# A four-layer graph network on one core: the second layer's input transposed by VectorE and through DRAM, the attention sources in another node order, the third layer's sum on GpSimd, and a new plan

## The chip, the cores and the metric

The kernel runs on one core of a Trainium2 chip. The core has five engines that run side by side and meet through semaphores: PE (TensorE, matrix products and their weight loads), DVE (VectorE), ACT (ScalarE), POOL (GpSimd) and SP (SyncE, which here only issues DMAs). The metric is the device time of one launch in microseconds, the median over the runs shown. One launch works through all 32 graphs.

## The reference, cut to what matters

Each of the 32 batch elements is a graph of 512 nodes with 128 features. All share one 0/1 adjacency `adj` (512x512, symmetric, with self loops). Four layers follow each other, each with a residual and a LayerNorm:

```python
x = _layernorm(x + _L0_gnn_ref(x, adj, ...))   # attention: softmax(leaky(s_i + d_j) + mask) @ (x W), leaky 0.3
x = _layernorm(x + _L1_gnn_ref(x, adj, ...))   # attention, then elu
x = _layernorm(x + _L2_gnn_ref(x, adj, ...))   # diag(A) x W[0] + offdiag(A) x W[1] + bias, A = rows of adj, softmaxed
x = _layernorm(x + _L3_gnn_ref(x, adj, ...))   # y = ((adj + I) x) W + bias; y / max(|y|, 1e-12)
```

The LayerNorm is `(x - mean) / sqrt(var + 1e-5)` over the 128 features. So each layer ends in 512 inverse square roots for each graph, and layer 3 in 512 more for its norm.

## The kernel before, in words

Names carry the layer as a digit (`pt1`, `nrm2`) and the graph as `@b`; lines are those of the profile.

**Tiling.** A graph's x is a tile of 128 partitions by 512: four chunks of 128 nodes side by side. Nearly all of the work is cut into *units*: small functions, each of which issues a few instructions on one engine. A table `PLAN` gives each unit and graph a place in one long order, `STARTS` does so for the work done once. The order is written out by the program as it stands, and each engine takes its own instructions in that order; semaphores hold an instruction back until its operands are there. The numbers in `PLAN` are places, not times (2648 of them before, 2980 after). Each tile is taken from a stock of its kind (`sq`: 30 tiles, `ps`: 6 banks of PSUM, and so on) when the first unit of that graph names it, and goes back after the last.

**Layers 0 and 1 (attention).** x has to be transposed first, so that features lie on the partitions. For layer 0, graphs 1 to 31 come in from DRAM by `lb` (four DMAs of short runs, L156), and DVE finishes the transposition in 32x32 blocks (`tr0`, L160). Graph 0, and layer 1 of every graph, is transposed by PE (`pt`, L167, four products with the identity) and copied out of PSUM by ACT (`xt`, L171). `ph` (PE, L179) gives xW with the source and target scores, `ex` (ACT, L183) their exponentials, and `h` (ACT, L189) the scaled rows. The score of the source has to lie along the free axis of every partition: for 27 of the 32 graphs DVE turns it (`rt`, L214), four small DMAs write it to DRAM (`rw`, L220), and one DMA reads it back to all partitions (`rb`, L224); for the other five PE does it (`pr`, L209). `al` (DVE, L236, four instructions of 128x512) forms the masked weights, `po` (PE, L196, 32 products for each layer) applies them. `rs`, `v0`, `lr`, `elu` (DVE) and `v1`, `exp` (ACT) finish the layer; `add` (POOL, L267) adds the residual.

**Layers 2 and 3 (aggregation).** `xh` (ACT, L273) and `xl` (POOL, L277) split x in a rounded part and the rest, `py` (PE, L284) multiplies both with the adjacency, `y` (ACT, L288) copies out, `po2` or `po3` (PE, L298, L299, L311) multiply with the weights. In layer 2 `v2` (DVE, L305) scales by 1/degree and adds `xb`, which is x plus the bias (POOL, L292). In layer 3 `v3` adds the bias (DVE, L315), `sq` squares and sums (ACT, L321), `ssp` takes the inverse root (POOL, L325 and L326), and `rr0` to `rr3` scale and add the residual (DVE, L333).

**The end of every layer.** `bn` (DVE, L340 and L342) gives mean and variance, `ms` (ACT, L346) turns the sign of the mean, `pw` (POOL, L350 and L351) raises the variance to the power -1/2 and multiplies, and `nrm` (ACT, L356) scales and shifts in four instructions. For example:

```python
nc.gpsimd.tensor_tensor(rn[:, 0], mv[:, :, 1], mhalf, op=ALU.pow)
nc.gpsimd.tensor_mul(rn[:, 1], mv[:, :, 0], rn[:, 0])
```

**Beginning and checks.** `e`, `am`, `m`, `mp` make the mask `em` and its transposes `mt` (float) and `mp` (bf16, in PSUM); `cva` copies `mt` to the two matrices of layers 2 and 3, and `cvd` corrects their diagonals. `de`, `dv` and `lp` test the assumptions under which this fast path holds, and `out_d` to `out_c` read out a flag at the end.

Of the kernel before, what the change touches and what calls it, by code (L numbers as in the profile page):

```python
# [18 lines left out]
P = 128  # L19
# [7 lines left out]
def kernel(  # L27
# [49 lines left out]
    an, em, mt = square("an"), square("em"), square("mt")  # L77
    eh = square("eh", BF16)
# [47 lines left out]
    kind("sq", 30, "x1 x2 x3 x4 o0 o1 o2 o3 t t3 xb y2 y3 xt0 xt1 xt2 tr0 tr1 tr2", plain([P, N]))  # L126
# [8 lines left out]
    kind("ss", 6, "ss", plain([P, NCH]))  # L135
    kind("rb", 4, "rb0 rb1", plain([P, N]))
# [21 lines left out]
    @unit("tr0", "sw0", "xt0")  # L158
    def _(b, sw, xt):
        nc.vector.transpose(xt, sw)  # L160

    for k in range(3):

        @unit(f"pt{k}", f"x{k}", f"pt{k}")
        def _(b, xk, p):
            for c in range(NCH):
                nc.tensor.transpose(p[:, c * P : (c + 1) * P], xk[:, c * P : (c + 1) * P], ident)  # L167

        @unit(f"xt{k}", f"pt{k}", f"xt{k}")
        def _(b, p, xt):  # L170
            nc.scalar.copy(xt, p)  # L171

    for k in range(2):
# [33 lines left out]
        def _(b, p, k=k):  # L207
            for c in range(NCH):
                nc.tensor.transpose(p[:, c * P : (c + 1) * P], exps[:, 2 * b + k, 0, c : c + 1].to_broadcast([P, P]), ident)  # L209
# [91 lines left out]
    @unit("v2", "po2", "xb", "o2")  # L301
    def _(b, p, xb, o):
        for c in range(NCH):
            cols = slice(c * P, (c + 1) * P)
            nc.vector.scalar_tensor_tensor(o[:, cols], p[:, cols], rdeg[:, c : c + 1], xb[:, cols], op0=ALU.mult, op1=ALU.add)  # L305

# [28 lines left out]
    for k in range(4):  # L335
# [8 lines left out]
        @unit(f"ms{k}", f"mv{k}")  # L344
        def _(b, mv):
            nc.scalar.mul(mv[:, :, 0], mv[:, :, 0], -1.0)  # L346

        @unit(f"pw{k}", f"mv{k}", f"rn{k}")
        def _(b, mv, rn):
            nc.gpsimd.tensor_tensor(rn[:, 0], mv[:, :, 1], mhalf, op=ALU.pow)  # L350
            nc.gpsimd.tensor_mul(rn[:, 1], mv[:, :, 0], rn[:, 0])  # L351
# [6 lines left out]

    @unit("st", "x4")
# [683 lines left out]
```

## Time and profile before

| | us |
|---|---|
| three runs | 580.44, 582.84, 582.96 (median 582.84) |
| the profiled execution | 582.73 |
| its span, first to last instruction | 581.0 |
| what lies around the span | 1.7 |
| busy: PE / DVE / ACT / POOL | 547.7 / 526.0 / 503.6 / 427.0 |

Busy times are the time in which at least one instruction of the engine was under way. Neighbours overlap in their pipelines, so the mean duration of a short instruction is longer than what it adds: four `nrm` instructions of 492 ns each take 1.55 us together. Group rows give `busy, mean ns of one`, and after the bar the idle time of the engine just before them, with what ended it.

### The profile page before, as it was taken

Reading aid. Unit: us, or ns where it says so; the run is one execution under the profiler, and the core shown is the slowest. Engines: PE = TensorE matmul, PEld = TensorE weight load, DVE = VectorE, ACT = ScalarE, POOL = GpSimd, SP = SyncE. Lnnn points to the kernel's source line nnn. Section 1 sums busy time; section 2 is a strip of 40 time slices with the busy share of each in tenths; the row PEclk is TensorE's granted clock in tenths of the full one; section 3 lists DMA queues with packets and bytes.
Section 4 is the critical chain, followed back from the end, with each engine's and each line's share of the span. In section 5 each row is a group of like instructions: output and inputs, shape, how many; then the busy total and the mean of one; then the engine's idle time right before and its main releaser. Section 6 shows DMA issues by size and latency. Waiting matters only on the chain.

```text
span 581.0 us, 13866 instructions
## 1 busy us (share of the span) xinstructions
PE 547.7 (94%) x4200; PEld 516.1 (89%) x4200; DVE 526.0 (91%) x2005; ACT 503.6 (87%) x1653; POOL 427.0 (73%) x578
## 2 busy tenths in 40 slices
PE   7799999899999999999999999999999999999980
PEld 6689999899999999999999989898998999998860
DVE  2688979899999999999998999999999999779674
ACT  4555598798989899999999889899988999998996
POOL 3151685787868787777878579776887779789985
PEclk9788999999999999999999999999999999999995
DMA  6616022323434334352432343332201111000013
GB/s 188 130 38 128 19 60 70 92 65 83 99 77 101 77 70 110 92 117 55 104 78 76 83 97 74 66 101 73 75 20 38 55 38 38 20 2 20 1 37 113
DMA packets 111296, 41.84 MB, mean 72 GB/s; under 512 B 69872, under 2 KB 103792, under 8 KB 111216
## 3 DMA queue, kind: packets, MB, share of 16 engines
q1 hardware_dynamic: 110640, 40.57, 29.2%
q8 instruction: 35, 0.57, 0.4%
q14 instruction: 45, 0.37, 0.2%
q10 hardware_dynamic: 576, 0.33, 0.2%
HBM read 32.38 MB, written 8.50 MB: 70 GB/s over the span
## 4 chain that ended last, share of the span: by engine, by line
DVE 35%; PE 33%; ACT 16%; POOL 5%; SPq 4%; issue 3%; DMA 2%; ACTq 0%; DVEq 0%; POOLq 0%
PE ps L196 16%; DVE al L236 12%; ACT sq L356 8%; PE ps L284 7%; DVE st L340 6%; PE ps L179 4%; DVE sq L333 3%; DVE sq L305 2%; SPq L156 2%; DVE mv L342 2%; DVE sq L243 2%; ACT hp L189 2%; PE ps L167 2%; PE ps L311 2%; DVE sq L253 2%
## 5 line engine op out<-in xcount | busy, mean ns | idle before, releaser
L196 PE MATMUL ps<-hp,al 128*128 128x129 f32 x2048 | 251.2, 279 | 6.4 <-DVE al L236 4.4
L196 PEld LDWEIGHTS ps<-hp,al 128*128 128x128 f32 x2048 | 243.1, 195 | 10.0 <-issue 3.1
L356 ACT ACTIVATE sq<-sq,rn 128x128 f32<-128x128 f32 x512 | 209.5, 492 | 12.8 <-POOL rn L351 12.6
L350 POOL TENSOR_TENSOR rn<-mv,mhalf 128x4 f32<-128x4 f32 x128 | 134.7, 1053 | 22.1 <-DVE mv L342 15.4
L236 DVE SCALAR_TENSOR_TENSOR al<-rb,exps,mp 128x512 f32<-128x512 f32 x216 | 145.5, 734 | 1.6 <-DMA rb<-rd 1.5
L340 DVE BATCH_NORM_STATS2 st<-sq 128x6 f32<-128x128 f32 x512 | 109.0, 273 | 4.2 <-POOL sq L267 4.1
L277 POOL TENSOR_TENSOR xr<-sq,xr 128x512 fp32r<-128x512 f32 x64 | 83.1, 1302 | 15.1 <-ACT xr L273 13.5
L189 ACT ACTIVATE hp<-ps,exps 128x128 f32<-128x128 f32 x256 | 87.8, 421 | 0.2
L179 PE MATMUL ps<-we,sq 128*128 128x131 f32 x512 | 73.5, 277 | 3.1 <-ACT sq L171 2.0
L179 PEld LDWEIGHTS ps<-we,sq 128*128 128x128 f32 x512 | 66.0, 190 | 5.9 <-ACT sq L171 2.6
L284 PE MATMUL ps<-off,xr 128*128 128x512 f32 x256 | 67.3, 405 | 1.8 <-ACT hp L189 1.5
L284 PE MATMUL ps<-a3t,xr 128*128 128x512 f32 x256 | 67.2, 405 | 0.7 <-ACT sq L249 0.7
L284 PEld LDWEIGHTS ps<-off,xr 128*128 128x128 f32 x256 | 45.7, 188 | 11.4 <-ACT hp L189 1.9
L284 PEld LDWEIGHTS ps<-a3t,xr 128*128 128x128 f32 x256 | 45.9, 188 | 10.2 <-ACT sq L249 1.0
L267 POOL TENSOR_TENSOR sq<-sq,x 128x512 f32<-128x512 f32 x32 | 42.3, 1323 | 15.6 <-DVE sq L253 10.4
L292 POOL TENSOR_TENSOR sq<-sq,bias_b 128x512 f32<-128x512 f32 x32 | 41.6, 1300 | 14.3 <-ACT sq L356 11.6
L333 DVE SCALAR_TENSOR_TENSOR sq<-sq,ss,sq 128x128 f32<-128x128 f32 x128 | 47.6, 413 | 3.7 <-POOL ss L326 3.6
L267 POOL TENSOR_TENSOR sq<-sq,sq 128x512 f32<-128x512 f32 x32 | 41.7, 1306 | 11.3 <-DVE sq L261 10.6
L298 PE MATMUL ps<-w,sq 128*128 128x128 f32 x256 | 49.5, 275 | 0.0
L299 PE MATMUL ps<-w,sq 128*128 128x128 f32 x256 | 49.5, 275 | 0.0
L342 DVE BATCH_NORM_AGGREGATE mv<-st 128x2 f32<-128x9 f32 x512 | 48.9, 155 | 0.0
L171 ACT COPY sq<-ps 128x512 f32<-128x512 f32 x65 | 37.8, 584 | 11.2 <-PE ps L167 10.9
(91 smaller groups left out, 832.9 us busy)
## 6 DMA issues: line engine op xcount, KB each, us to landing
rb<-rd SPq DMA_DIRECT2D x54, 256.0 KB
x<-in_x_dram SPq DMA_DIRECT2D x32, 256.0 KB
out_dram<-sq SPq DMA_DIRECT2D x32, 256.0 KB
sw<-in_x_dram SPq DMA_DIRECT2D x124, 64.0 KB
rd<-rt SPq DMA_DIRECT2D x216, 0.5 KB
an<-in_adj_dram SPq DMA_DIRECT2D x3, 256.0 KB
an<-in_adj_dram ACTq DMA_DIRECT2D x1, 256.0 KB
w<-in_L_gnn_W_dram SPq DMA_DIRECT2D x2, 64.0 KB
```

The lines of the kernel that those rows point to most:

```text
L179: nc.tensor.matmul(twos(p)[:, c, :FE], xt[:, (2 * half + c) * P : (2 * half + c + 1) * P], ATT[k], start=True, stop=True)
L189: nc.scalar.activation(h[:, 2 * half + c, :F], twos(p)[:, c, :F], AF.Identity, bias=pc if k else 0.0, scale=pc)
L196: nc.tensor.matmul(twos(p)[:, c, : F + 1], al[:, j, rows], h[:, j, :], start=(j == 0), stop=(j == NCH - 1))
L236: nc.vector.scalar_tensor_tensor(al[:, j, :], r, exps[:, 2 * b + k, 2, j : j + 1], mask[:, j, :], op0=ALU.max, op1=ALU.mult)
L267: nc.gpsimd.tensor_add(o, o, xk)
L277: nc.gpsimd.tensor_sub(xl, xk, xh.bitcast(F32))
L284: nc.tensor.matmul(p, part[:, j * P : (j + 1) * P], mat[:, j, :], start=(i + j == 0), stop=(i + j == NCH))
L333: nc.vector.scalar_tensor_tensor(o[:, cols], o[:, cols], ss[:, c : c + 1], x3[:, cols], op0=ALU.mult, op1=ALU.add)
L340: nc.vector.bn_stats(st[:, c, :6], o[:, c * P : (c + 1) * P])
L342: nc.vector.bn_aggr(mv[:, c, :], st[:, c, :])
L350: nc.gpsimd.tensor_tensor(rn[:, 0], mv[:, :, 1], mhalf, op=ALU.pow)
L356: nc.scalar.activation(xo[:, c * P : (c + 1) * P], o[:, c * P : (c + 1) * P], AF.Identity, bias=rn[:, 1, c : c + 1], scale=rn[:, 0, c : c ...
```

## The change

- **Layer 1's transposition** leaves PE and ACT for 27 of the 32 graphs (3 to 29). DVE transposes 32x32 blocks (`tr1`), one DMA writes the tile to DRAM (`tw1`), four DMAs read it back (`tb1`).
- **Node order.** In layers 0 and 1 the source nodes stand in another order (`swapped`: 32-node blocks regrouped) in the transposed x, the scores and the mask. `rw` becomes one DMA instead of four. The old order is kept for layers 2 and 3: `en` copies the mask back on POOL, `an` transposes it (16 PE products), `cva` reads these.
- **Layer 2's sum.** `v2` on DVE is gone: ACT scales out of PSUM (`o2s`), POOL adds (`v2p`).
- **Logarithms.** Every power -1/2 on POOL (`pw`, `ssp`) and every `ms` is gone. ACT takes `Ln` (`le`) and `Exp` with scale -0.5 (`lx`), DVE multiplies with the negated mean (`nm`); in layer 3 `sm` (DVE), `sle`, `slx` (ACT) do the norm. One table is loaded at the start by number.
- **Normalisation.** `nrm0` and `nrm2` move from ACT to POOL (`nrm0p`, `nrm2p`); `nrm1` and `nrm3` stay.
- **Beginning.** Graphs 0 to 3 are transposed by PE, whole tiles are loaded for them and `lb` starts with graph 4. `warm2` (8 dummy products) is gone, `de` and `lpp` come later.
- **End.** For graphs 30 and 31 everything from `y3` on goes chunk by chunk; the copy of `y3` is shared by ACT and DVE, and DVE normalises two of the four chunks (`nvc1`, `nvc3`). The units not shown below (`v3c`, `sqc`, `smc`, `slc`, `sxc`, `bnc`, `lec`, `lxc`) are those of the whole tile on one chunk.
- **Plan.** All places in `PLAN` and `STARTS` are new; `sq` has 33 tiles instead of 30.

```diff
+    ej = square("ej")
...
-    kind("sq", 30, "x1 x2 x3 x4 o0 o1 o2 o3 t t3 xb y2 y3 xt0 xt1 xt2 tr0 tr1 tr2", plain([P, N]))
+    kind("sq", 33, "x1 x2 x3 x4 o0 o1 o2 o3 t t3 xb y2 y3 xt0 xt1 xt2 tr0 tr1 tr2", plain([P, N]))
...
+    kind("dt", 4, "dt1", lambda name: dram.tile([P, N], F32, name=name))
...
+    def swapped(t):
+        return t.rearrange("p (a c i) -> p c a i", a=NCH, c=NCH)
...
-        nc.vector.transpose(xt, sw)
+        nc.vector.transpose(swapped(xt), sw)
...
-        def _(b, xk, p):
-            for c in range(NCH):
-                nc.tensor.transpose(p[:, c * P : (c + 1) * P], xk[:, c * P : (c + 1) * P], ident)
+        def _(b, xk, p, k=k):
+            for c in range(NCH):
+                dst = swapped(p)[:, c] if k < 2 else p[:, c * P : (c + 1) * P]
+                nc.tensor.transpose(dst, xk[:, c * P : (c + 1) * P], ident)
...
+    @unit("tr1", "x1", "tr1")
+    def _(b, x1, tr):
+        nc.vector.transpose(tr.rearrange("p (f c i) -> p c f i", f=NCH, c=NCH), x1)
+    @unit("tw1", "tr1", "dt1")
+    def _(b, tr, dt):
+        nc.sync.dma_start(dt, tr)
+    @unit("tb1", "dt1", "xt1")
+    def _(b, dt, xt):
+        for f in range(4):
+            src = bass.AP(tensor=dt.tensor, offset=dt.offset + f * P, ap=[[N, Q], [Q * N, P // Q], [1, P]])
+            nc.sync.dma_start(xt[f * Q : (f + 1) * Q, :].rearrange("p (a n) -> p a n", n=P), src)
...
-                nc.tensor.transpose(p[:, c * P : (c + 1) * P], exps[:, 2 * b + k, 0, c : c + 1].to_broadcast([P, P]), ident)
+                nc.tensor.transpose(swapped(p)[:, c], exps[:, 2 * b + k, 0, c : c + 1].to_broadcast([P, P]), ident)
...
-            for a in range(P // Q):
-                src = bass.AP(tensor=rt.tensor, offset=rt[a * Q : (a + 1) * Q].offset, ap=[[R * Q, NCH], [1, Q]])
-                nc.sync.dma_start(rd.rearrange("(c a i) -> a c i", c=NCH, a=P // Q)[a], src)
+            nc.sync.dma_start(rd.rearrange("(q i) -> q i", i=Q), rt[::R, :])
...
-    @unit("v2", "po2", "xb", "o2")
-    def _(b, p, xb, o):
-        for c in range(NCH):
-            cols = slice(c * P, (c + 1) * P)
-            nc.vector.scalar_tensor_tensor(o[:, cols], p[:, cols], rdeg[:, c : c + 1], xb[:, cols], op0=ALU.mult, op1=ALU.add)
...
-    @unit("ssp", "ss")
+    @unit("sm", "ss")
     def _(b, ss):
-        nc.gpsimd.tensor_scalar(ss, ss, 1e-24, None, op0=ALU.max)
-        nc.gpsimd.tensor_tensor(ss, ss, mhalf, op=ALU.pow)
+        nc.vector.tensor_single_scalar(ss, ss, 1e-24, op=ALU.max)
+    @unit("sle", "ss")
+    def _(b, ss):
+        nc.scalar.activation(ss, ss, AF.Ln)
+    @unit("slx", "ss")
+    def _(b, ss):
+        nc.scalar.activation(ss, ss, AF.Exp, scale=-0.5)
...
-        @unit(f"ms{k}", f"mv{k}")
-        def _(b, mv):
-            nc.scalar.mul(mv[:, :, 0], mv[:, :, 0], -1.0)
-        @unit(f"pw{k}", f"mv{k}", f"rn{k}")
+        @unit(f"le{k}", f"mv{k}", f"rn{k}")
         def _(b, mv, rn):
-            nc.gpsimd.tensor_tensor(rn[:, 0], mv[:, :, 1], mhalf, op=ALU.pow)
-            nc.gpsimd.tensor_mul(rn[:, 1], mv[:, :, 0], rn[:, 0])
+            nc.scalar.activation(rn[:, 1], mv[:, :, 1], AF.Ln)
+        @unit(f"lx{k}", f"rn{k}")
+        def _(b, rn):
+            nc.scalar.activation(rn[:, 0], rn[:, 1], AF.Exp, scale=-0.5)
+        @unit(f"nm{k}", f"mv{k}", f"rn{k}")
+        def _(b, mv, rn):
+            nc.vector.scalar_tensor_tensor(rn[:, 1], mv[:, :, 0], -1.0, rn[:, 0], op0=ALU.mult, op1=ALU.mult)
...
+        @unit(f"nrm{k}p", f"o{k}", f"rn{k}", f"x{k + 1}")
+        def _(b, o, rn, xo):
+            for c in range(NCH):
+                nc.gpsimd.tensor_scalar(xo[:, c * P : (c + 1) * P], o[:, c * P : (c + 1) * P], rn[:, 0, c : c + 1],
+                                        rn[:, 1, c : c + 1], op0=ALU.mult, op1=ALU.add)
+    @unit("o2s", "po2", "o2")
+    def _(b, p, o):
+        for c in range(NCH):
+            cols = slice(c * P, (c + 1) * P)
+            nc.scalar.activation(o[:, cols], p[:, cols], AF.Copy, scale=rdeg[:, c : c + 1])
+    @unit("v2p", "xb", "o2")
+    def _(b, xb, o):
+        nc.gpsimd.tensor_add(o, o, xb)
+    @unit("y3x", "py3", "y3")
+    def _(b, p, y):
+        nc.scalar.copy(y[:, : 2 * P], p[:, : 2 * P])
+    @unit("y3y", "py3", "y3")
+    def _(b, p, y):
+        nc.vector.tensor_copy(y[:, 2 * P :], p[:, 2 * P :])
+    for c in range(NCH):
+        cols = slice(c * P, (c + 1) * P)
+        @unit(f"po3c{c}", "y3", "po3")
+        def _(b, y, p, cols=cols):
+            nc.tensor.matmul(p[:, cols], y[:, cols], w3_s, start=True, stop=True)
...
+        @unit(f"rrc{c}", "ss", "x3", "o3")
+        def _(b, ss, x3, o, c=c, cols=cols):
+            nc.vector.scalar_tensor_tensor(o[:, cols], o[:, cols], ss[:, c : c + 1], x3[:, cols], op0=ALU.mult, op1=ALU.add)
...
+        @unit(f"nmc{c}", "mv3", "rn3")
+        def _(b, mv, rn, c=c):
+            nc.vector.scalar_tensor_tensor(rn[:, 1, c : c + 1], mv[:, c, 0:1], -1.0, rn[:, 0, c : c + 1], op0=ALU.mult, op1=ALU.mult)
+        @unit(f"nrc{c}", "o3", "rn3", "x4")
+        def _(b, o, rn, xo, c=c, cols=cols):
+            nc.scalar.activation(xo[:, cols], o[:, cols], AF.Identity, bias=rn[:, 1, c : c + 1], scale=rn[:, 0, c : c + 1])
+        @unit(f"nvc{c}", "o3", "rn3", "x4")
+        def _(b, o, rn, xo, c=c, cols=cols):
+            nc.vector.tensor_scalar(xo[:, cols], o[:, cols], rn[:, 0, c : c + 1], rn[:, 1, c : c + 1], op0=ALU.mult, op1=ALU.add)
+        @unit(f"stc{c}", "x4")
+        def _(b, x4, c=c, cols=cols):
+            nc.sync.dma_start(out[b, c * P : (c + 1) * P, :], x4[:, cols])
...
-        nc.scalar.activation(bad[:, 0:1], minus1, AF.Exp)
+        nc.scalar.add_instruction(mybir.InstLoadActFuncSet(name=nc.get_next_instruction_name(), act_func_set_id=6))
...
-            nc.tensor.transpose(p[:, :P], ident, ident)
-    @unit("warm2", "pf")
-    def _(b, p):
-        for i in range(8):
...
-            nc.vector.tensor_single_scalar(em[:, c, :], an[:, c, :], 0.0, op=ALU.is_gt)
+            nc.vector.tensor_single_scalar(swapped(ej[:, c, :]), an[:, c, :].rearrange("p (c a i) -> p c a i", c=NCH, a=NCH), 0.0, op=ALU.is_gt)
...
-        @unit(f"cva{c}")
+        @unit(f"en{c}")
         def _(b, c=c):
-            nc.scalar.copy(off[:, c, :], mt[:, c, :])
-            nc.scalar.copy(a3t[:, c, :], mt[:, c, :])
+            nc.gpsimd.tensor_copy(em[:, c, :].rearrange("p (c a i) -> p a c i", c=NCH, a=NCH), ej[:, c, :].rearrange("p (a c i) -> p a c i", c=NCH, a=NCH))
+        @unit(f"an{c}", f"pn{c}")
+        def _(b, p, c=c):
+            for ic in range(NCH):
+                nc.tensor.transpose(p[:, ic * P : (ic + 1) * P], em[:, ic, c * P : (c + 1) * P], ident)
+        @unit(f"cva{c}", f"pn{c}")
+        def _(b, p, c=c):
+            nc.scalar.copy(off[:, c, :], p)
+            nc.scalar.copy(a3t[:, c, :], p)
...
-        "ja": 1, "warm": 2, "wb": 3, "awt0": 4, "warm2": 5, "awc0": 6, "e2": 7, "e0": 10, "rest": 11, "am2": 12,
-        "e1": 13, "awq0": 14, "aws0": 16, "am0": 17, "e3": 18, "eh": 20, "am1": 21, "awt1": 22, "am3": 23,
-        "awc1": 24, "m2": 26, "m3": 27, "awq1": 29, "m0": 30, "m1": 31, "cva2": 33, "aws1": 34, "mp": 35, "cva1": 38,
-        "cvd2": 39, "de": 42, "cva3": 45, "cvd1": 46, "cvd3": 48, "cva0": 51, "cvd0": 54, "dga": 55, "deg": 61,
-        "lpp": 239, "lpd": 274, "dv": 420, "out_d": 2455, "out_p": 2530, "out_c": 2533,
+        "ja": 1, "warm": 2, "rest": 6, "awt0": 7, "awc0": 9, "e2": 10, "awq0": 12, "e0": 13, "am2": 14, "en2": 15,
+        "e1": 16, "e3": 17, "am0": 18, "aws0": 19, "am1": 20, "eh": 22, "wb": 24, "am3": 27, "m1": 29, "m2": 30,
+        "m0": 32, "m3": 33, "en1": 36, "mp": 38, "en0": 42, "en3": 46, "awt1": 52, "awc1": 58, "dga": 61, "an2": 65,
+        "awq1": 68, "cva2": 70, "aws1": 71, "deg": 73, "an3": 75, "an1": 78, "cvd2": 79, "cva3": 80, "cva1": 86,
+        "an0": 87, "cvd3": 89, "cva0": 90, "cvd1": 93, "cvd0": 97, "lpp": 274, "lpd": 301, "dv": 374, "de": 458,
+        "out_d": 2690, "out_p": 2697, "out_c": 2703,
...
```

## The prediction

> **What bounds the kernel now.** I read the busy shares first, then the table of stretches, then the chain, and last the groups that the change touches. From the page and the table of stretches (columns: stretch, its length, busy us and count of PE, PEld, DVE, ACT, POOL, then clock, DMA share, GB/s):
>
> ```profile
> span 581.0 us, 13866 instructions
> PE 547.7 (94%) x4200; PEld 516.1 (89%) x4200; DVE 526.0 (91%) x2005; ACT 503.6 (87%) x1653; POOL 427.0 (73%) x578
> DVE 35%; PE 33%; ACT 16%; POOL 5%; SPq 4%; issue 3%; DMA 2%; ACTq 0%; DVEq 0%; POOLq 0%
> ```
>
> ```profile
> 0.00:10.00 10.00, 7.39 (x41) 6.99 (x42) 2.04 (x11) 2.07 (x3) 2.44 (x22) 1.00 0.70 215
> 10.00:20.00 10.00, 7.23 (x51) 6.28 (x50) 6.11 (x14) 9.17 (x24) 5.03 (x10) 0.77 0.79 158
> ...
> 200.00:250.00 50.00, 49.27 (x381) 46.52 (x380) 48.93 (x193) 46.70 (x156) 41.29 (x54) 1.00 0.34 86
> ...
> 550.00:560.00 10.00, 9.95 (x59) 8.54 (x58) 7.87 (x34) 10.00 (x38) 8.63 (x11) 1.00 0.10 29
> 560.00:570.00 10.00, 4.26 (x28) 3.36 (x26) 9.16 (x41) 9.68 (x47) 8.91 (x15) 0.91 0.24 73
> 570.00:581.00 11.00, 0.00 (x0) 0.00 (x0) 3.52 (x24) 6.66 (x19) 4.62 (x7) 0.50 0.36 106
> ```
>
> From 60 to 500 us PE is busy for 433 of 440 us and DVE for 427: two engines bound this stretch together. DVE's 55 us of idle time split into 19.5 (0 to 60), 13.2 (60 to 500) and 22.3 (500 to 581). At the end PE is done by 566.5, and ACT and POOL carry what is left. So it counts how much PE loses, what DVE's total becomes, and what becomes of both ends.
>
> The groups (busy and mean ns of one | idle before), then single instructions in order of time, then one line's durations (min/median/max):
>
> ```profile
> L350 POOL TENSOR_TENSOR rn<-mv,mhalf 128x4 f32<-128x4 f32 x128 | 134.7, 1053 | 22.1 <-DVE mv L342 15.4 <-DVE rt L214 4.2 <-DVE rs L200 2.3
> L305 DVE SCALAR_TENSOR_TENSOR sq<-ps,rdeg,sq 128x128 f32<-128x128 f32 x128 | 35.4, 337 | 4.6 <-PE ps L299 4.6
> L383 POOL TENSOR_SCALAR nident<-ident 128x128 f32<-128x128 f32 x1 | 0.3, 301 | 0.1
> ```
>
> ```profile
> 526.86 1.29 POOL L292 TENSOR_TENSOR sq<-sq,bias_b 128x512 f32<-128x512 f32 x1
> 527.77 0.40 DVE L511 SCALAR_TENSOR_TENSOR bad<-bad 128x1 f32<-128x1 f32 x1
> 14.24 0.42 DVE L500 TENSOR_REDUCE ends<-eb 128x1 f32<-128x256 f32 x1 [2.15 <-DMA eb<-in_L_gnn_e_dram]
> ```
>
> ```profile
> L333 DVE SCALAR_TENSOR_TENSOR sq<-sq,ss,sq x128: 302/343/1446, 121.9 to 572.0; 128x128 f32<-128x128 f32 x128
> ```
>
> L511 works on one element, has two operands in SBUF, starts while POOL's sum runs, and ends 0.02 us after it. The same happens to L333: median 343 ns, up to 1446. L305 has one operand in PSUM, and its mean is its floor.
>
> **What the Trainium skill says.** "SBUF — State Buffer", section "SBUF: two separate sides", says that a DVE instruction with two SBUF inputs and a GpSimd instruction that reads SBUF share one port pair, held by one for the whole instruction. The trace agrees for POOL's 128x512 sums (L511 above), but not for the power: 75 instances of L333 overlap mostly with L350 and have a median of 340 ns, so 1 us on four elements blocks nothing. "ScalarE: Activation LUTs", section "Table sets: the hidden batching unit", says that one set holds both exp and ln, so that changing between them loads nothing; the kernel before uses no Ln, so no run here shows it, and its single table load took 1.28 us. "GPSIMD Engine Reference", section "Engine selection", puts one-input work near line rate and two-input work at half of it; the trace agrees: 301 ns for a one-input 128x128 (L383), 457 for a two-input one (L461).
>
> **The change part by part.**
>
> *PE.* 27 units `pt1` go: 39.0 us / 64 (L167) = 0.61 each, -16.5. Three `pt0` come, +1.8; the 16 products of `an` at 0.16 (L444), +2.6; `warm2` goes, -1.9. Sum -14, to **534**.
>
> *DVE.* I count distances from start to start, since short instructions overlap. `v2` goes: 32 x 1.03 (four L305 in the chain) = -33. `nm` comes, 126 + 8 chunks: a reciprocal (L200) adds 0.09, I take 0.10, +13.4. `sm`: 38 x 0.09 = +3.4. `tr1`: 27 x 0.62 (L160) = +16.7; three `tr0` less, -1.9. Chunked ends (eight `v3c` for two `v3`, four `nvc`, two `y3y`): +2.5. Sum +1, to **527**, without blocking.
>
> *Blocking, the unknown that decides.* Before, `rr`, `lr` and `elu` (192 instructions, two SBUF operands) pay 9.9 + 2.5 + 2.1 = 14.5 us over their floors (means 413, 751 and 737 ns against some 336, 672 and 670 where POOL stands still). After, `nm` adds 134 such instructions and `v2p` adds 32 POOL sums to 160. A sum blocks for about 1.1 us (1446 - 343). In the plan's own order (5.2 places per us) only 4 of 128 `rr` stand within 1.1 us after a POOL sum before, 9 after: the order avoids it there. But 38 of the 134 `nm` do, and what is left of these sums adds up to 18.5 us. Nothing in the trace shows `nm` itself. Lower bound 0 (an `nm` that finds POOL idle, as POOL waits for it in layers 0 and 2); upper bound 35 (134 x 0.15 and twice the old 14.5). I take **+20**: DVE 547.
>
> *ACT.* `ms` -128 x 0.11, `nrm0` and `nrm2` -64 x 1.55, 24 fewer `xt` at 0.5, that is -125; `le`, `lx`, `sle`, `slx` 344 x 0.15 (between L346's 0.11 and 0.21, most wait for their neighbour) = +52; `o2s` 32 x 1.2 (L249) = +38. To about 468, off the path: its cover is DVE and PE.
>
> *POOL.* L350, L351, L326, L325: -134.7 - 31.2 - 33.8 - 8.1 = -208. `v2p` 32 x 1.3 (L267) = +42. `nrm0p` and `nrm2p`: 256 instructions, not shown with pointers; between 0.30 (L383) and 0.46 (L461), I take 0.35, +90. `en` +3. To 354, off the path even at 0.46 (381).
>
> *SP and DRAM.* A middle graph issues 1 + 1 + 4 + 8 + 2 = 16 DMAs before (`ld`, `st`, `lb`, `rw`, `rb`), 15 after (`rw` 2, `tw1` 1, `tb1` 4), at about 0.5 us each. `tb1` waits for `tw1`, and behind it on SP wait `rb`, `lb` and `st`. A 256 KB landing takes 3.1 to 3.4 us (`rb` in the chain). The way is 3.3 + 4 x 0.5 + 3.3 = 8.6 us; the plan leaves at least 3.3 + 5.6, in the median 4.4 + 14.3 (places / 5.2). Cost taken: 0, hidden behind other graphs; bounds 0 and 13 (27 x 0.5). The node order itself changes no count; a strided write at 32-element runs could cost DVE or PE, 0 to 0.1 us in each of 55 `tr` units, taken as 0.
>
> *Beginning.* `al0@0` starts at 15.28 because `de` (L500 above) waits for `eb`; PE was ready at 13.4: -1.9. Graphs 1 to 3 no longer wait for `lb`. DVE's idle 19.5 becomes about 15.
>
> *End.* DVE's 22.3 us there are waits on ACT and POOL, with 1.05 us powers in sequence. These go, and the chunks shorten the last way: 11 short steps, some 3 us, 0.8 of hand-overs and 4 of the store (0.5 issue, 3.3 landing). But DVE still has 10 us of chunk work, with gaps. I take 7 to 8 of idle time, of which 3.3 is the store. In the middle PE drops from 98% to about 96% busy, so DVE waits less for it: 13.2 becomes 5.
>
> *Sum.* 527 + 20 + (15 + 5 + 7.5) = 574.5, and 1.7 around the span: **576 us** against 582.73 of the profiled execution, which is 0.1 below the median 582.84.
>
> **The rivals.**
>
> 1. *PE bounds, DVE is blocked little.* For it: L333's median shows most instructions unhindered, and the plan keeps `rr` clear. Against it: 38 `nm` behind sums. PE 534 + 9 (beginning) + 6 + 11 (from its last product to the end, 14.5 before) = 560, with 1.7: **562**.
> 2. *Blocking costs more than all gains (slower).* Place: `nm` and `rr` on DVE against POOL's sums and the new `nrm0p`, `nrm2p`, since an order worked out in advance slips. From over 29 us of it the result is above 585.7; at 35, DVE 562 + 27.5 + 1.7 = **591**. For it: L511's single element was held. Against it: `lr` and `elu`, which POOL waits for, paid 0.07 each.
> 3. *The way through DRAM is late.* `ph1`, then `al1` wait, at 13 us: **589**. Against it: the median gap of 18.7 us against 8.6.
> 4. *DVE stays as scarce as it was:* its idle time remains at 34 in place of 27.5, **583**, no change. For it: DVE was at 97% in the middle already.
>
> **How the numbers follow.** A measurement here can tell about 0.5% (2.9 us) from no change. Chances: the forecast 0.45 (565 to 587), rival 1 0.22, rival 2 0.18, rival 3 0.05, rival 4 0.10. Faster: 0.36 + 0.22 = 0.58. Same: 0.07 of the forecast + 0.07 (rival 4) + 0.02 (rival 2) = 0.16. Slower: 0.02 + 0.16 (rival 2) + 0.05 + 0.03 = 0.26. The range 558 to 592 runs from rival 1 with some room to rival 2; its ends come from blocking at 0 and at 35 us. The forecast's own range is 565 to 587.
>
> **What would show it.** In the profile after: PE near 534, ACT below 480, POOL below 390, DVE near 547 and the busiest engine in the middle; one table load; `nm` with a mean clearly over its minimum, and a maximum over 1 us; no `ph1` waiting for a DMA; the first `al` near 13.4; the span's end about 11 us after PE's last product. The forecast is wrong if DVE's total stays under 532 or passes 560, if `nm` is never held, or if `ph1` or `al1` wait for `xt1` for many microseconds.

## The result, and the profile after

The changed kernel takes **597.64 us** (median of four runs, 596.81 to 599.65), the kernel before 581.98 in the same series: a ratio of **1.0277** (95% interval 1.0239 to 1.0314). The change makes it slower by about 16 us, where 576.0 was forecast. The profiled execution took 597.39 us, with a span of 595.6, so 1.8 us lie around it.

The page after, in the same three lines (span; busy time, share and count of each engine; engines on the chain that ended last):

```profile
span 595.6 us, 13866 instructions
PE 543.9 (91%) x4112; PEld 504.4 (85%) x4112; DVE 556.1 (93%) x2085; ACT 459.0 (77%) x1712; POOL 390.1 (66%) x550
DVE 64%; ACT 11%; PE 11%; issue 4%; DMA 4%; SPq 3%; POOL 2%; ACTq 0%; DVEq 0%; POOLq 0%
```

DVE's busy time has risen by 30 us and its share of the chain from 35 to 64%; PE, ACT and POOL all have less to do. The table of stretches after (columns as in the prediction) shows where DVE is full:

```profile
0.00:60.00 60.00, 52.73 (x436) 51.10 (x437) 45.34 (x143) 32.52 (x106) 25.55 (x64) 1.00 0.46 108
60.00:500.00 440.00, 417.57 (x3200) 389.12 (x3199) 438.07 (x1629) 343.89 (x1278) 308.39 (x420) 1.00 0.39 103
200.00:250.00 50.00, 48.25 (x366) 44.64 (x365) 49.89 (x179) 40.90 (x157) 36.42 (x50) 1.00 0.45 121
500.00:595.60 95.60, 73.60 (x479) 64.19 (x478) 72.71 (x315) 82.61 (x330) 56.17 (x68) 0.91 0.12 34
```

From 60 to 500 us DVE is busy for 438 of 440 us (427 before). From 200 to 250 us it is busy for 49.89 of 50 us, but with 179 instructions where the kernel before got through 193 in 48.93 us. The mix of instructions is another one, so this alone doesn't say that any of them became longer. The groups of instructions do (busy, mean ns of one | idle before):

```profile
L352 DVE SCALAR_TENSOR_TENSOR sq<-sq,ss,sq 128x128 f32<-128x128 f32 x120 | 60.5, 545 | 0.0
L373 DVE SCALAR_TENSOR_TENSOR rn<-mv,rn 128x4 f32<-128x4 f32 x126 | 37.8, 310 | 6.0 <-ACT rn L369 5.7
L384 POOL TENSOR_SCALAR sq<-sq,rn 128x128 f32<-128x128 f32 x256 | 117.6, 475 | 29.3 <-DVE rn L373 23.9 <-issue 1.5 <-DVE rs L220 1.3
```

L352 is `rr` (L333 before, mean 413 ns); L373 is the new `nm`; L384 is GpSimd's new normalisation. The two DVE lines read two operands in SBUF. Their durations (min/median/max):

```profile
L373 DVE SCALAR_TENSOR_TENSOR rn<-mv,rn x126: 107/149/1728, 28.7 to 578.9; 128x4 f32<-128x4 f32 x126
```

```profile
L352 DVE SCALAR_TENSOR_TENSOR sq<-sq,ss,sq x120: 298/339/1506, 121.1 to 575.1; 128x128 f32<-128x128 f32 x120
```

Medians are at the floor (the shortest usual duration), means far above it: a minority takes much longer, up to 1.5 and 1.7 us. By count in the trace, 26 of the 120 `rr` last over 0.5 us (11 of 128 before) and 38 of the 126 `nm` over 0.25 us. The timeline of all engines shows one such place (start us, us; only DVE's and POOL's lines of it):

```profile
538.05 0.16 DVE L621 SCALAR_TENSOR_TENSOR bad<-bad 128x1 f32<-128x1 f32 x1
...
538.50 1.67 POOL L295 TENSOR_TENSOR xr<-sq,xr 128x512 fp32r<-128x512 f32 x1 [0.97 <-ACT xr L291]
...
538.93 2.92 DVE L352 SCALAR_TENSOR_TENSOR sq<-sq,ss,sq 128x128 f32<-128x128 f32 x3
540.12 1.31 POOL L285 TENSOR_TENSOR sq<-sq,sq 128x512 f32<-128x512 f32 x1
```

Three `rr` in a row need at most 1.0 us by the median. Here they take 2.92, and two POOL sums of two operands lie over them. Where no sum runs, four take 1.16:

```profile
551.90 1.16 DVE L352 SCALAR_TENSOR_TENSOR sq<-sq,ss,sq 128x128 f32<-128x128 f32 x4
```

L621, the single element that took 404 ns before, meets no sum here and takes 158.

### The profile page after: what moved, and what is told of

The parts are those of the page before. It is cut to its first block, busy times and chain, and to the rows that moved or that the text cites. A ratio compares the mean times of both kernels' runs of the same rounds, so it can differ in the third digit from the quotient of the medians.

```text
span 595.6 us, 13866 instructions
## 1 busy us (share of the span) xinstructions
PE 543.9 (91%) x4112; PEld 504.4 (85%) x4112; DVE 556.1 (93%) x2085; ACT 459.0 (77%) x1712; POOL 390.1 (66%) x550
## 4 chain that ended last, share of the span: by engine, by line
DVE 64%; ACT 11%; PE 11%; issue 4%; DMA 4%; SPq 3%; POOL 2%; ACTq 0%; DVEq 0%; POOLq 0%
DVE al L254 19%; DVE st L359 11%; DVE sq L352 7%; PE ps L216 6%; DVE mv L361 4%; DVE sq L261 4%; ACT sq L378 3%; DVE rn L373 3%; DVE sq L271 3%; DVE sq L279 3%; ACT sq L333 2%; DVE sq L181 2%; DVE sq L165 2%; PE ps L199 2%; DVE sq L327 1%
## 5 line engine op out<-in xcount | busy, mean ns | idle before, releaser
L216 PE MATMUL ps<-hp,al 128*128 128x129 f32 x2048 | 246.9, 275 | 6.9 <-ACT hp L209 2.3
L216 PEld LDWEIGHTS ps<-hp,al 128*128 128x128 f32 x2048 | 238.3, 191 | 13.4 <-ACT hp L209 3.6
L384 POOL TENSOR_SCALAR sq<-sq,rn 128x128 f32<-128x128 f32 x256 | 117.6, 475 | 29.3 <-DVE rn L373 23.9
L378 ACT ACTIVATE sq<-sq,rn 128x128 f32<-128x128 f32 x248 | 102.4, 491 | 13.9 <-DVE rn L373 13.1
L359 DVE BATCH_NORM_STATS2 st<-sq 128x6 f32<-128x128 f32 x504 | 107.0, 270 | 3.4 <-POOL sq L285 1.8
L365 ACT ACTIVATE rn<-mv 128x4 f32<-128x4 f32 x126 | 26.8, 217 | 47.9 <-DVE mv L361 33.2
L285 POOL TENSOR_TENSOR sq<-sq,x 128x512 f32<-128x512 f32 x32 | 41.6, 1300 | 33.4 <-DVE sq L271 16.2
L285 POOL TENSOR_TENSOR sq<-sq,sq 128x512 f32<-128x512 f32 x32 | 41.3, 1291 | 30.3 <-DVE sq L279 15.0
L352 DVE SCALAR_TENSOR_TENSOR sq<-sq,ss,sq 128x128 f32<-128x128 f32 x120 | 60.5, 545 | 0.0
L395 POOL TENSOR_TENSOR sq<-sq,sq 128x512 f32<-128x512 f32 x32 | 42.6, 1330 | 22.9 <-ACT sq L391 13.8
L267 ACT ACTIVATE sq<-ps,rs 128x128 f32<-128x128 f32 x128 | 39.1, 367 | 20.9 <-DVE rs L220 19.7
L316 PE MATMUL ps<-w,sq 128*128 128x128 f32 x256 | 49.9, 277 | 2.6 <-ACT sq L306 2.6
```

The costliest lines, as they stand in the source:

```text
L216: nc.tensor.matmul(twos(p)[:, c, : F + 1], al[:, j, rows], h[:, j, :], start=(j == 0), stop=(j == NCH - 1))
L285: nc.gpsimd.tensor_add(o, o, xk)
L316: nc.tensor.matmul(p[:, cols], y[:, cols], w21, start=True, stop=False)
L352: nc.vector.scalar_tensor_tensor(o[:, cols], o[:, cols], ss[:, c : c + 1], x3[:, cols], op0=ALU.mult, op1=ALU.add)
L359: nc.vector.bn_stats(st[:, c, :6], o[:, c * P : (c + 1) * P])
L378: nc.scalar.activation(xo[:, c * P : (c + 1) * P], o[:, c * P : (c + 1) * P], AF.Identity, bias=rn[:, 1, c : c + 1], scale=rn[:, 0, c : c ...
```

## The experiments

**The theory:** DVE's instructions with two SBUF operands wait for POOL's sums at the shared port of which the prediction speaks (below: waits for the port), and these waits are the loss. **Rivals:** the work itself is too much for DVE, the way through DRAM is late, or the new order and its end stall. Differences are taken against 597.64 us; the kernel before, run beside each group, came to 581.1 to 582.2 us each time.

**1. `nm` with one operand in PSUM** (the mask `mp`, which is always there; the scaling of the mean by 1/std is left out):

```diff
-            nc.vector.scalar_tensor_tensor(rn[:, 1], mv[:, :, 0], -1.0, rn[:, 0], op0=ALU.mult, op1=ALU.mult)
+            nc.vector.scalar_tensor_tensor(rn[:, 1], mv[:, :, 0], -1.0, mp[:, 0, :NCH], op0=ALU.mult, op1=ALU.mult)
```

> The changed kernel, but nm (L373) takes its second operand from the mask in PSUM instead of rstd in SBUF; so the mean is not scaled with rstd. Same count, order and waits on ACT. Theory 'blocking' (DVE bounds the middle, and its instructions with two SBUF operands stand still while a 128x512 sum runs on POOL): the mean of nm falls from 310 ns to about 150, DVE's busy time from 556 to about 537, the time from 597.6 to 578 to 584. Rival 'count' (DVE has simply more instructions, each at its own length): nm stays at 310 and the time within 3 us of 597.6. Rival 'end' (the last 95 us set the loss, ACT and chains bound them): nm gets shorter, and the time falls by less than 6 us.

Measured: 584.92 us (ratio to before 1.0048, 1.0031 to 1.0065), that is -12.7, 0.9 short of the theory's range, with DVE at 539.4 busy. The group rows of `nm` and of `rr` in this run:

```profile
L373 DVE SCALAR_TENSOR_TENSOR rn<-mv,mp 128x4 f32<-128x4 f32 x126 | 16.2, 138 | 7.1 <-ACT rn L369 6.9
L352 DVE SCALAR_TENSOR_TENSOR sq<-sq,ss,sq 128x128 f32<-128x128 f32 x120 | 61.6, 555 | 0.0
```

The instruction stays and only an operand changes place: `nm`'s 37.8 us become 16.2. `rr` stays about as long (545 before the edit).

**2. `rr` as well** (its residual also replaced by the mask, so layer 3's residual of 30 graphs is left out):

```diff
-            nc.vector.scalar_tensor_tensor(o[:, cols], o[:, cols], ss[:, c : c + 1], x3[:, cols], op0=ALU.mult, op1=ALU.add)
+            nc.vector.scalar_tensor_tensor(o[:, cols], o[:, cols], ss[:, c : c + 1], mp[:, c, cols], op0=ALU.mult, op1=ALU.add)
```

> As x1_nm_psum, and rr (L352) too takes its second tensor from the mask in PSUM instead of x3: the residual of layer 3 is left out for 30 of the 32 graphs. Blocking: the mean of rr falls from 545 to about 340 ns, DVE's busy time to about 513, so that PE (544) bounds: 568 to 576 us. Count: no change against the changed kernel beyond 3 us. End: as x1_nm_psum, or up to 8 us less since rr stands in the end.

Measured: **562.47 us** (0.9661, 0.9645 to 0.9677), that is -35.2, more than was expected. The page's line of busy times and the group row of `rr`:

```profile
PE 531.7 (95%) x4112; PEld 500.8 (89%) x4112; DVE 516.9 (92%) x2085; ACT 456.4 (81%) x1712; POOL 384.8 (69%) x550
```

```profile
L352 DVE SCALAR_TENSOR_TENSOR sq<-sq,ss,mp 128x128 f32<-128x128 f32 x120 | 34.9, 334 | 0.0
```

As many instructions on each engine as after the change, DVE 39.2 us shorter, and PE the fullest engine. The result is 20 us faster than the kernel before, but parts of the work are left out (run 4 makes the fairer comparison). One objection stays: `rr` no longer needs `x3` here, so its tile comes free earlier.

**3. Three of the four `rr`** of a graph take the mask, on top of run 1, and the fourth still reads `x3`, which answers that objection:

```diff
-            nc.vector.scalar_tensor_tensor(o[:, cols], o[:, cols], ss[:, c : c + 1], x3[:, cols], op0=ALU.mult, op1=ALU.add)
+            nc.vector.scalar_tensor_tensor(o[:, cols], o[:, cols], ss[:, c : c + 1], (mp[:, c, cols] if c < 3 else x3[:, cols]), op0=ALU.mult, op1=ALU.add)
```

> As the run with nm's second operand in PSUM (584.9 us, scaling of the mean left out), and of the four additions rr of a graph three take PSUM's mask and only the fourth reads x3, so x3 is needed and kept as long as in the new kernel (the residual of layer 3 is left out for three quarters of the nodes). It tells apart why the run with all four in PSUM came to 562.5. Theory (the wait for the shared port): 90 of 120 additions fall from about 0.55 to 0.335 us, three quarters of those 22.5 us come, 565 to 571 us. Rival (x3's buffer came free earlier, and its wait was gone): at most a few us come, 578 to 585.

Measured: 573.07 us (0.9876, 0.9823 to 0.9929), 11.9 less than run 1, between the two expectations. The group rows tell why:

```profile
L352 DVE SCALAR_TENSOR_TENSOR sq<-sq,ss,mp 128x128 f32<-128x128 f32 x90 | 27.3, 334 | 0.0
L352 DVE SCALAR_TENSOR_TENSOR sq<-sq,ss,sq 128x128 f32<-128x128 f32 x30 | 21.2, 709 | 0.0
```

The 30 that still read SBUF twice are the ones that waited longest already: by the trace of run 1 the same 30 took 629 ns there, where all 120 took 555. Here they take 709; that they now meet sums that another `rr` would have sat out is likely, but not shown. So the 90 exempt instructions bring 13 us of DVE's busy time and not the 20 that 90 x (555 - 334) would give, and the time follows DVE's busy time (-14.3 against -11.9). With `x3` kept as long as before, 24.6 of run 2's 35.2 us have come. The other 10.6 lie between this run and run 2, where the last 30 `rr` lose 30 x (709 - 334) = 11 us as well, so little is left for an early free tile.

**4. The same edit in the kernel before** (`rr` with the mask; its residual left out for all 32 graphs):

> The kernel before, but rr takes its second tensor from the mask in PSUM: layer 3's residual is left out. It takes away the 10 us that rr is held before. Blocking with PE as second bound: PE is busy for 98% of the middle, so of the 10 us at most half comes back: 576 to 581 us. If DVE alone bounds the kernel before: 572 us.

Measured: 575.13 us (0.9876, 0.9846 to 0.9905): -6.1 (0.9 more than was expected), with DVE 9.6 us less busy. The kernel before pays for the same waits of `rr`, about a quarter as much as the changed one: 6.1 us against the 22.5 between runs 1 and 2. Without the waits of `rr` in either, and of `nm` in the changed kernel, that one is faster by 12.7 us (562.47 against 575.13).

**5. `nm` on GpSimd**, with nothing left out: ACT turns the sign of the mean, POOL multiplies.

```diff
             nc.scalar.activation(rn[:, 1], mv[:, :, 1], AF.Ln)
+            nc.scalar.mul(mv[:, :, 0], mv[:, :, 0], -1.0)
...
-            nc.vector.scalar_tensor_tensor(rn[:, 1], mv[:, :, 0], -1.0, rn[:, 0], op0=ALU.mult, op1=ALU.mult)
+            nc.gpsimd.tensor_mul(rn[:, 1], mv[:, :, 0], rn[:, 0])
```

> The changed kernel, nothing left out: the product of nm for 126 of the 134 cases goes to POOL (one 128x4 product, about 0.2 us as L351 before), the mean's sign to ACT beside le. Blocking: DVE loses nm's 37.8 us, POOL gains 25 of instructions that block nothing; DVE about 520, rr still held (about 545 ns): 580 to 588 us. Rival 'plan' (the order is made for nm on DVE; POOL's own queue holds the small product behind sums and normalisations, and nrm waits): over 595 us.

Measured: 584.97 us (1.0056, 1.0033 to 1.0078), -12.7. The theory's range holds. The whole of `nm` leaves DVE (530.5 busy), and no more comes back than in run 1, where the same 126 instructions stayed without their wait. So moving the work gained nothing over taking away the wait; whether the new work on POOL (413.3 us busy, 390.1 in the kernel after) took something back is not shown.

**6. `rr` with one operand in PSUM, with nothing left out:** for the 23 graphs for which a bank can be spared, layer 3's product gets its bias in PSUM and stays there.

```diff
+    @unit("v3p", "po3")
+        nc.vector.tensor_tensor(chunks(p), chunks(p), bc(bias3_b), op=ALU.add)
...
+        @unit(f"rp{c}", "po3", "ss", "x3", "o3")
+            nc.vector.scalar_tensor_tensor(o[:, cols], p[:, cols], ss[:, c : c + 1], x3[:, cols], op0=ALU.mult, op1=ALU.add)
```

> The changed kernel, nothing left out: for 23 of the 32 graphs layer 3's y stays in its PSUM bank (v3 adds the bias there, sq and rr read it there), so that rr has one operand in SBUF. Blocking: rr of these graphs falls to about 335 ns, DVE loses 23/30 of 25 us = 19: 578 to 586 us. Rival 'banks' (the bank is held longer, and PE waits for it): 595 us or more, with waits of PE on rr.

Measured: 595.95 us (1.0241, 1.0221 to 1.0261), only -1.7, the rival's side, though DVE lost 13.5 us of busy time. In the waits of DVE, and in those of PE (us in total, times, longest):

```profile
DVE rs L220 <- PE ps L216: 11.1, 13, 2.7
```

```profile
PE ps L199 <- ACT hp L209: 3.9, 3, 2.2
PE ps L302 <- ACT hp L209: 3.8, 2, 2.0
```

DVE now waits for PE: 11.1 us, 2.5 in the kernel after. Of PE's two waits for ACT the first was 2.8 us and the second is new; in all PE stands idle no longer than in the kernel after (50.7 us against 51.7). The wait of PE for `rr` that the rival named was seen once, for 2.4 us.

**7. The bank held, the wait kept:** only the last quarter of the product stays in PSUM until its `rr`; the bank is occupied as long as in run 6, and 23 instructions are exempt.

```diff
+        nc.vector.tensor_tensor(chunks(o)[:, :3, :], chunks(p)[:, :3, :], bc(bias3_b)[:, :3, :], op=ALU.add)
+        nc.vector.tensor_tensor(p[:, 3 * P :], p[:, 3 * P :], bias3_b, op=ALU.add)
```

> The new kernel, but for 23 graphs the last quarter of layer 3's product stays in its PSUM bank until its rr has read it there; the other three quarters go to SBUF as before and rr reads them there. The bank is held as long as in the run with the whole product in PSUM (595.95 us), while only 23 additions are spared the wait (about -4.6 us on VectorE, +1.5 for the split addition of the bias). Theory (that run's 13.5 us of VectorE were eaten by the banks): 601 to 609 us. Rival (banks cost nothing, VectorE's time there was not on the path): 593 to 598.

Measured: 605.98 us (1.0425, 1.0369 to 1.0481), +8.3 with DVE at 554.2, within the theory's range. Holding banks in this order costs some 10 us (estimate: 8.3, and the 2 us by which DVE's busy time fell), about as much as run 6 should have won. That run 6 lost its gain to the banks is the likely reading of the two runs; the waits name no bank.

**8. Runs 5 and 6 together, and without `sm`** (the floor 1e-24 becomes the bias of ACT's logarithm):

> x9_nm_pool and x10_rr_psum together, and sm is gone (its floor of 1e-24 is added as ACT's bias in sle): nothing left out beyond rounding. Blocking: nearly all waiting of DVE gone, DVE about 500, PE bounds: 564 to 574 us, faster than both kernels. Rival 'plan' or 'banks': 585 us or more.

Measured: 581.64 us (1.0009, 0.9999 to 1.0019), equal to the kernel before, and far from the theory's 564 to 574. With DVE at 509.0 and PE at 536.9 no engine is full over the whole span, so what holds this version up is not its busy time; it stays open. **Run 5 without `sm` alone:**

> The new kernel with nm's product on GpSimd (as in the run that came to 585 us) and without sm: the floor under the sum of squares is added as a bias in ScalarE's logarithm. Theory: 7.1 us of sm and some of the 5.5 us that VectorE waits for sm's input leave VectorE; its busy time falls from 530 to about 523 and the time to 577 to 581 us, level with the kernel before. Rival (PE, 542 us at 93%, has become the bound): 584 to 586, nothing gained.

Measured: 583.27 us (1.0018, 1.0004 to 1.0032). 6.4 us of DVE's busy time gave 1.7: between the two expectations, nearer the rival. No version that leaves nothing out came below the kernel before.

**9. `rr` off DVE:** on top of the last run, ACT scales and POOL adds, as layer 2 does.

```diff
+            nc.scalar.activation(o[:, cols], o[:, cols], AF.Copy, scale=ss[:, c : c + 1])
...
+        nc.gpsimd.tensor_add(o, o, x3)
```

> A version meant to beat both, with nothing left out: nm's product on GpSimd, no sm, and rr of 30 graphs as ScalarE's scaling (120 x about 0.38 = 45 us) and one GpSimd sum each (30 x 1.33 = 40 us), so that VectorE has almost no instruction left that reads two SBUF operands: VectorE near 467 us, ScalarE 513, GpSimd 457, PE 535 to 540. Theory (waits for the port were the loss; PE bounds): 566 to 578 us. Rival (the statistics of layer 3 now wait for GpSimd's sum, in an order made for VectorE's): 588 or more.

Measured: 596.74 us (1.0269, 1.0219 to 1.0320), the rival's side, though DVE fell to 483.1. DVE's waits in this run (us in total, times, longest):

```profile
DVE st L370 <- POOL sq L286: 14.4, 13, 2.2
...
DVE st L370 <- POOL sq L356: 11.4, 5, 4.2
...
DVE st L370 <- POOL sq L407: 9.6, 7, 2.9
```

L370 is `bn`, which DVE now starts only when POOL has delivered; L356 is the new sum, the others are sums of old. The wait for the port was traded for a wait for data.

**10. Three parts of the change undone one at a time.** Layer 1's transposition back on PE and ACT, at the places of `tr1` and `tw1`:

```diff
+    for b in range(3, 30):
+        PLAN["pt1"][b], PLAN["xt1"][b] = PLAN["tr1"][b], PLAN["tw1"][b]
```

> One part undone: layer 1's x of graphs 3 to 29 is again transposed by TensorE and copied out by ScalarE, at the places in the order where the new kernel has VectorE's transposition and the DRAM write. Theory (VectorE's work and its held instructions set the time): VectorE loses 27 x 0.689 = 18.6 us, PE gains 108 products (about 15 us, to some 559), ScalarE 27 evictions of about 0.48 = 13 us, and the time falls by most of the 18.6: 580 to 588 us. Rival A (the DRAM way was late after all): more than 18.6 us come back, below 579. Rival B (PE's and PSUM's burden was the reason to move it: PE then waits for banks): 594 or more.

Measured: 594.02 us (1.0201, 1.0172 to 1.0229), -3.6; DVE -14.1, PE +7.9 and ACT +12.5 us busy. It is neither of the first two cases, and just inside the third, but not by waits of PE for banks: it is DVE that waits more, 7.2 us for PE (2.5 in the kernel after) and 9.7 for ACT before `nm` (5.7). So DVE's spared time mostly becomes waiting, and nothing here shows the way through DRAM to cost more than a few us. Layer 2's sum back on DVE (`v2` at the places of `o2s`, no `v2p`):

> One part undone: layer 2's sum is one scaled addition on VectorE again (128 instructions), ScalarE's scaling (128 x 0.380 = 49 us less on ScalarE, some of it in the older place) and GpSimd's 32 sums of 1.33 us are gone. Theory: VectorE has about 33 us more, and 42.6 us fewer of the two-input sums that hold it back, worth some 8 to 12 us of its 50: VectorE near 578 us, the time 612 to 622. Rival (GpSimd's sums cost VectorE as much as they took off it): 590 to 600.

Measured: 614.87 us (1.0566, 1.0520 to 1.0612), +17.2, as expected. In its group rows

```profile
L352 DVE SCALAR_TENSOR_TENSOR sq<-sq,ss,sq 128x128 f32<-128x128 f32 x120 | 55.1, 501 | 0.1
...
L373 DVE SCALAR_TENSOR_TENSOR rn<-mv,rn 128x4 f32<-128x4 f32 x126 | 30.9, 255 | 7.3 <-ACT rn L369 7.2
```

the waits shrink by 12 us with 160 in place of 192 sums, but the 35 us of `v2` weigh more: in this order moving it was right. The last two graphs whole instead of in chunks:

> One part undone: the last two graphs' layer 3 is done whole, not in chunks. Theory (chunks are worth the 3 us by which the time from PE's last product to the end fell, and cost VectorE 2.5): 598 to 602 us. Rival (the chunks' many small instructions on ScalarE and VectorE are what stretched the end from 500 us on by some 8 us): 588 to 594.

Measured: 599.66 us (1.0286, 1.0250 to 1.0321), +2.0, as expected: the chunks are worth about 2 us.

**11. Two misses that tell little of the theory.** POOL subtracts the mean itself, so that `nm0` and `nm2` go:

```diff
-                nc.gpsimd.tensor_scalar(..., rn[:, 0, c : c + 1], rn[:, 1, c : c + 1], op0=ALU.mult, op1=ALU.add)
+                nc.gpsimd.tensor_scalar(..., mv[:, c, 0:1], rn[:, 0, c : c + 1], op0=ALU.subtract, op1=ALU.mult)
```

> The changed kernel, but POOL's normalisation in layers 0 and 2 subtracts the mean and then multiplies with rstd, so that nm is not needed there: 62 nm instead of 126, nothing else moved, nothing left out. Blocking: DVE loses 64 x 0.31 = 20 us, half of it waiting, 578 to 584 us. Count: 64 x 0.15 = 10 us of DVE, 587 to 590 us. End: less than 6 us gained, 592 or more.

Measured: 626.32 us (1.0755, 1.0737 to 1.0773). All three expectations missed. The same instruction with another pair of operations is far slower:

```profile
L384 POOL TENSOR_SCALAR sq<-sq,mv,rn 128x128 f32<-128x128 f32 x256 | 211.8, 840 | 11.4 <-DVE sq L261 4.3 <-issue 2.9 <-ACT rn L365 2.7
```

94 us more of POOL work hide whatever the missing `nm` gave. And the powers back on POOL (`nrm0`, `nrm2` back on ACT, no logarithms), in the new order:

> The changed kernel with the power -1/2 on POOL, the sign on ACT and nrm0 and nrm2 on ACT as before, in the places of lx, nm, le and the POOL normalisation; the transposition by DVE and DRAM, the node order, the new beginning, layer 2's sum on POOL and the chunked end of graphs 30 and 31 stay. Blocking: nm and sm are gone (DVE 556 to about 510), the powers keep POOL on instructions that block nothing, so rr is held less; ACT at about 505, POOL at about 440: 575 to 585 us, the remaining blocks giving the upper end. End: the powers come one after another on POOL again, 590 to 600 us.

Measured: 650.23 us (1.1165, 1.1141 to 1.1189), outside both ranges. DVE's busy time fell to 527.8, but ACT waits 38.4 us for POOL's `rn`: probably because the order was laid out for other durations. Neither run speaks for or against the theory.

**12. The end: layer 1's normalisation of graphs 27 to 31 on POOL**, in the kernel after, then on top of run 8's first version:

```diff
+    for b in [27, 28, 29, 30, 31]:
+        PLAN["nrm1p"][b], PLAN["nrm1"][b] = PLAN["nrm1"][b], -1
```

> The new kernel, with layer 1's normalisation of the last five graphs on GpSimd instead of ScalarE, at the same places in the order. VectorE still has 21 us of idle time in the last 80 us, where 7.5 were forecast for the whole end, and ScalarE is busy 93 of the 100 us from 480 to 580. Theory (ScalarE's work is what the end waits for): ScalarE loses 5 x 1.54 = 7.7 us there, GpSimd gains 5 x 1.9, and 3 to 7 us of the time go: 591 to 595 us. Rival (the order and the waits for the port set the end, ScalarE is only full, or GpSimd's slower normalisation takes the place): 596 to 601.

Measured: 603.45 us (1.0401, 1.0349 to 1.0453).

> The same end on the version with nm's product on GpSimd, without sm, and with rr's operand kept in PSUM for 23 graphs (581.6 us); nothing is left out. Theory (ScalarE in the end): 576 to 579 us, faster than the kernel before. Rival: 581 to 585.

Measured: 591.10 us (1.0152, 1.0095 to 1.0209). They are slower by 6 and 9 us than what they start from, beyond the theory's range and the rival's: taking work from ACT in this way doesn't shorten the time.

## Why the prediction was wrong

The sum of the prediction, term by term, against the profiled execution (us):

| term | forecast | measured |
|---|---|---|
| DVE's work without waits for the port | 512.5 (526 + 1 - 14.5) | 506.5 (556.1 - 49.6) |
| waits for the port | 34.5 (14.5 + 20) | 49.6 |
| DVE idle: beginning, middle, end | 15, 5, 7.5 | 14.7, 1.9, 22.9 |
| around the span | 1.7 | 1.8 |
| sum | 576.2 | 597.4 |

The waits are each group's count times its mean over its floor: `nm` 126 x (310 - 147) = 20.5, `rr` 120 x (545 - 338) = 24.8, and `sm`, `lr`, `elu` about 4.3.

Two terms make the error: the waits, +15.1, and the end, +15.4. The work (-6.0) and the middle (-3.1) took back 9 of these.

**The first step that failed is "Blocking", and in it one term.** It put +20 on `nm`: 38 `nm` behind sums, 18.5 us. That is the size that came (38 that took over 0.25 us, 20.5 us), in part by luck: only 23 of these 38 are among the 38 that the order names. But it left `rr` at its old 9.9 us, since "the order avoids it there" with 9 close behind a sum. In the run 26 of 120 took over 0.5 us, and `rr` paid 24.8. None of the 9 is among the 26. Set beside the order, 24 of the 26 met a sum that stands *behind* them in it (6 of 11 in the kernel before), and two met mostly an L384. The prediction counted only the sums that stand ahead. But a place says where an instruction is issued, not when it runs: POOL was already at the later sum when DVE came to the `rr`. It is not that `nm`'s waits alone pushed DVE back: in run 1, where they are gone, `rr` still takes 555 ns. The new sums of layer 2 are a part of it, 501 ns without them (run 10); why DVE stands so far behind POOL in this order stays open. Runs 1 to 3 show that this waiting, and not the work, is what makes the change a loss: without it in `nm` and `rr` the kernel takes 562.47 us.

**The second is "End".** 7 to 8 us of idle time were forecast after the powers had gone. It stayed as before. The end of the table of stretches, in four steps of 20 us, after the change and then in run 2:

```profile
515.60:535.60 20.00, 19.47 (x149) 17.96 (x148) 13.93 (x59) 19.77 (x75) 14.41 (x18) 1.00 0.08 23
535.60:555.60 20.00, 18.44 (x119) 15.93 (x116) 15.57 (x62) 17.02 (x62) 16.09 (x18) 1.00 0.09 27
555.60:575.60 20.00, 15.03 (x85) 12.16 (x85) 17.89 (x79) 18.86 (x81) 13.18 (x19) 0.96 0.13 40
575.60:595.60 20.00, 5.49 (x18) 3.99 (x17) 11.76 (x63) 11.70 (x62) 0.76 (x1) 0.59 0.19 55
```

```profile
481.10:501.10 20.00, 19.93 (x156) 18.64 (x155) 15.33 (x79) 19.80 (x73) 14.06 (x15) 1.00 0.10 29
501.10:521.10 20.00, 19.71 (x131) 17.41 (x131) 13.59 (x60) 19.58 (x69) 17.74 (x22) 1.00 0.05 14
521.10:541.10 20.00, 16.84 (x102) 13.73 (x100) 15.27 (x84) 19.53 (x89) 13.64 (x20) 1.00 0.18 53
541.10:561.10 20.00, 4.96 (x22) 3.26 (x22) 12.04 (x67) 12.60 (x64) 1.30 (x1) 0.68 0.19 56
```

DVE's column adds up to 59.2 and 56.2 of 80 us: it stands idle for 20.8 and 23.8 us, with or without the waits for the port (22.3 in the kernel before). The prediction had assumed that this idle time goes with the powers; it did not. ACT is busy for 55.7 and 58.9 of the first 60 us, but run 12, which relieves it, got slower; what sets the end stays open. From the start of the last `al` to the end it is 68.4 us before, 76.2 after, 75.0 in run 1 and 71.1 in run 2: 5 of the 8 us that were added go with the waits for the port, and 3 are not explained.

**What else the prediction said, point by point.**

- *PE to 534:* 543.9 in the kernel after, 531.7 in run 2, with the same 4112 products. The count was right, but the same products took 12 us more busy time in the kernel after, where PE also stands idle for longer (51.7 us, 29.4 in run 2). The forecast had not reckoned with that.
- *DVE near 547, the busiest in the middle:* 556.1, and it is. Its work came out 6 us lower than forecast, which no run pins to one term.
- *ACT 468, below 480:* 459.0. *One table load:* yes, at the start, 1283 ns; exp and ln alternate without another. That agrees with what was cited from the Trainium skill, "ScalarE: Activation LUTs", section "Table sets: the hidden batching unit".
- *POOL 354, at most 381:* 390.1. The normalisation was taken at 0.35 us and bounded by 0.46; it is 475 ns, so 256 of them are 32 us more. Bound and value were read from instructions with constants (L383) and with two tensors (L461), and none with two pointers was there to read. These two, 301 and 457 ns, stand at 1 to 1.5 and not at the 1 to 2 with which the prediction calls them in agreement.
- *SP and DRAM, cost 0:* right in what it said. The write takes 2.2 us, each read 2.1 (3.3 were taken), and among the waits no `ph1` waits for a DMA. Undoing layer 1's transposition gave 3.6 us.
- *Beginning:* first `al` at 13.5 (13.4 forecast), idle 14.7 (15). *From PE's last product to the end:* 11.6 us (11).
- *Rivals:* rival 1 (562) is what run 2 measures once the waits of `nm` and `rr` are gone, with PE at 95%. Rival 2 named the mechanism, both lines and the side, with a chance of 0.18. At its 35 us of added waits, which is what came, it gave 591; the idle end adds 15, and the lower work and the fuller middle take 9 of that back. Rival 3 fell. Rival 4's 583 fell too, but its idle time of 34 us for DVE was nearer to the measured 39.5 than the forecast's 27.5.

The upper end of the range took the added waits at 35 us, as they came, but kept the hoped-for end.

## What to carry to other kernels

Before work is put on VectorE beside GpSimd, list every VectorE instruction with two operands in SBUF and price each by what it pays when it meets a GpSimd sum, old ones included: `rr`, whose instruction the change did not touch, waits for 24.8 us, more than the new `nm`, and 15 of these are new. An order of issue is no measure of that where one engine runs behind another: look at the sums that stand after the instruction, too. An operand in PSUM takes the wait away without taking the work away, and that is also the test (126 instructions, 310 ns to 138); but a bank held for it has its own price, here some 10 us by estimate, and no version with nothing left out beat the kernel before. And don't expect idle time to go with the instruction named beside it: the idle end stood at 21 to 24 us with and without the powers and the waits.

## What the runs showed of the hardware

- **How small an instruction can be and still wait:** `nm` has four elements for each partition and took up to 1728 ns. Its 47 instances that started while a sum ran ended 0.02 us after that sum (median). `sm`, with one tensor operand, waits too (121 to 1243 ns). This agrees with the Trainium skill, "GPSIMD Engine Reference", section "Key points", which names two-port modes of VectorE beside two SBUF inputs.
- **Which GpSimd instructions hold VectorE:** its two-operand sums of 128x512 do. The 25 `rr` that started while one ran took 1.36 us in the median and ended 0.15 us after it. The one-operand L384 shows less of it: the 12 `rr` that met L384 and no sum took 340 ns in the median, as the 50 did that met nothing, and one of them 537, to 0.14 us after the end of L384. The other way round, L384 waits too: six that met an `lr` or `elu` at their start took 752 to 957 ns, where the median is 453. The Trainium skill, "SBUF — State Buffer", section "SBUF: two separate sides", lets any GpSimd instruction that reads SBUF hold the port for its whole length. For the sums this trace agrees, for L384 in these few instances, and for the power in the kernel before (1.05 us) it does not: of 81 `rr` that met a power and no sum the longest took 354 ns.
- **GpSimd's tensor_scalar with two pointers, 128x128:** multiply and add 475 ns, subtract and multiply 840.
